# Neighbour lists of the first half moved into layer 1, and four tiles instead of six in the first phase

## The chip, the cores and the metric

The kernel runs on one core of one Trainium2 chip. The metric is the device time of one execution in microseconds (us); the time of a kernel is the median of its runs. A profile is one execution that the hardware profiler recorded; its span runs from its first to its last instruction, and the execution's own time is a little longer.

## The reference: two layers over one graph

There are N = 4096 nodes with 512 features each, and one dense matrix `adj` (4096 x 4096, float32), of which under 1% is not zero (each entry, its mirror and the diagonal).

```python
# layer 0
h = maximum(layernorm(x), 0)
d = where(rowsum > 0, rowsum ** -0.5, 0)          # rowsum = adj.sum(axis=1)
x = x + relu((d[:, None] * adj * d[None, :]) @ h @ W0 + b0)
# layer 1
h = maximum(layernorm(x), 0)
e = leaky_relu(h @ W @ a[:F] + (h @ W @ a[F:]).T, 0.2)
att = softmax(where(adj > 0, e, -1e12), axis=1)
neg = -softmax(where(adj > 0, -e, -1e12), axis=1)
x = x + elu(concatenate([att @ h, neg @ h], axis=1) @ wtrans)
```

Layer 0 is a dense product. Layer 1 needs, for each row, only the rows of `h` that `adj` marks.

## The kernel before

**Layer 0, first phase (lines 922 to 983).** The 4096 rows are 32 tiles of 128. For each row tile j the kernel loads the row of `adj` (four pieces of 512 KB, on SP's queue) and sums it for `d` (three pieces on ScalarE, one on VectorE), normalizes and transposes the tile of x (`turn_x`, matmuls at line 648), multiplies it by W0 (`project`, line 679) and scales it into `y0[j]`, which stays in SBUF. In the same loop a few columns of the result are accumulated plainly: `GROUPS[0]` names the first tile and the number of tiles, six before, and `multiply` (line 852) does one 128x512 matmul for each of them and each j. Each of these tiles holds one of the eight PSUM banks through the phase; the projections and transposes use those left. The part of `adj_t` for these columns is loaded for each j.

**Layer 0, the other groups (`group`, lines 1032 to 1083).** Each entry (i0, n) of `GROUPS` after the first is n tiles of output, over 16 steps `jp` of two row tiles. Here the product of 2x2 blocks is formed with seven products in place of eight (line 893, 128x256 matmuls): per step and pair of tiles seven matmuls. The left-hand sums of blocks of `adj_t` are made on VectorE (`sum_at`, lines 880 to 883). The results of the group before are finished during the first steps (`finish0`): residual, layer norm, the two scalar products s and t of a row for layer 1, and the row written to DRAM, on GpSimd's and ScalarE's queues, into eight tables, so that layer 1 can gather from each of them.

**Masks and lists.** Layer 1 works on 64 blocks of 64 rows, two blocks to a pair. `pack` turns each loaded part of `adj_t` into a byte mask, writes it to the tables behind the rows, and leaves a flag for each block and neighbour. A group in `EARLY` has its part of `adj_t` loaded and masked beforehand, in the group that the dictionary names by its index, and once more for its own product. `make_lists(g)` makes the neighbour lists of one half of the blocks (g = 0 or 1). `make_keys` transposes flags on TensorE (line 552) and forms sort keys and counts. Then 60 rounds (`list_round`: an eight-fold maximum at line 391 and a replacement at line 393) sort them, `make_places` finds where each list begins, and 24 joins (line 413, indirect DMAs from GpSimd) write pieces to DRAM. `deal` reads them back as indices with three DMAs. The units of this work stand in two queues in Python, `listing` and `joining`, from which `step(jp)` takes a few in each step of a group: that sets the order of the program around the change. Each engine takes its instructions in the order in which the program issues them to it.

**Layer 1 (`sparse_layer1`, lines 1236 to 1380).** The first pair, 16, is worked on within the last group of layer 0. For the others a loop over 62 blocks does, at block k, the `product` of block k (14 matmuls of 128x512, two records each in the profile, line 1296), asks for the gathers of a pair two further on (`gather`, line 451: 22 indirect DMAs on GpSimd in chunks of 8, 6 and 8), makes the weights of block k + 2 on VectorE and ScalarE (lines 463 to 493), turns the block before, and at every second block multiplies a finished pair by `wtrans` (`finish1`, line 1319). There are two sets of three buffers for gathered rows. The blocks begin with the second half's (pair 17 on), so that the lists of half g = 1 are needed first and those of g = 0 only from pair 0 on, after 15 pairs. `judge` compares counts, and on a bad verdict a dense version of layer 1 would run; it does not here.

Of the kernel before, what the change touches and what calls it, by code (L numbers as in the profile page):

```python
# [8 lines left out]
F32 = mybir.dt.float32  # L9
# [3 lines left out]
BF16 = mybir.dt.bfloat16  # L13
AF = mybir.ActivationFunctionType
ALU = mybir.AluOpType
# [4 lines left out]
P = 128  # L20
IB = 512


GROUPS = ((26, 6), (16, 4), (20, 4), (0, 4), (4, 4), (8, 4), (12, 4), (24, 2))

EARLY = {(24, 2): (2,), (12, 4): (3,), (8, 4): (4,)}
PAIR0 = 16
# [232 lines left out]
def gcn_gat_kernel(  # L260
# [159 lines left out]
    def deal(g):  # L420

        src = lst_dram[g].rearrange("(b n) o -> b (n o)", n=STR)
        k = 0
        for n in CHUNKS:
            nc.gpsimd.dma_start(
                out=idx[g][:, :, k : k + n],
                in_=src[:, k * P : (k + n) * P].rearrange("b (p k) -> p b k", k=n),
            )
            k += n

    def mean_var(pool, xt, name, pin):
# [14 lines left out]

    def gather(gt, n, a):

        c = sum(CHUNKS[:a])
        for k in range(CHUNKS[a]):  # L450
            nc.gpsimd.indirect_dma_start(  # L451
                out=gt[:, k, :],
                out_offset=None,
                in_=table[2 * n // RPT],
                in_offset=bass.IndirectOffsetOnAxis(
                    ap=idx[n // NH][:, n % NH, c + k : c + k + 1], axis=0
                ),
            )

    def scores(s, z, t):  # L460
# [53 lines left out]

    late_mask = ctx.enter_context(sbuf(name="late_mask", bufs=1, side="right"))
    late_m = late_mask.tile([P, EJ, TT * P], U8, name="late_m")
    with sbuf(name="y0", bufs=1) as y_pool, sbuf(name="wa", bufs=1) as wa_pool, sbuf(name="bits", bufs=4) as bits_pool, sbuf(name="small0", bufs=4) as small, ExitStack() as rest, ExitStack() as lists:
        list_pool = lists.enter_context(sbuf(name="list", bufs=1, side="right"))
        rank = list_pool.tile([P, EN], F32, name="rank")
        nc.gpsimd.iota(  # L520
            rank, [[-1, EN]], base=EN, channel_multiplier=0, allow_small_or_imprecise_dtypes=True
        )
        before = list_pool.tile([P, NE + 1, NH], F32, name="before")
        nc.gpsimd.memset(before[:, 0, :], 0.0)
        for e in range(NE):
            nc.vector.tensor_tensor(
                before[:, e + 1, :], before[:, e, :], ident[:, e * NH : (e + 1) * NH], ALU.add
            )
        start = list_pool.tile([NH, 1], F32, name="start")
        nc.gpsimd.iota(  # L530
            start, [[0, 1]], base=0, channel_multiplier=STR, allow_small_or_imprecise_dtypes=True
        )
        flags = [list_pool.tile([P, EJ * NE, 2 * NH], BF16, name=f"flags{g}") for g in range(2)]
        keys, lst = {}, {}
# [214 lines left out]
        def affine(y, acc, j):  # L749

            nc.vector.scalar_tensor_tensor(y, acc, d_all[:, j : j + 1], b_bc, ALU.mult, ALU.add)
            return y

        def new_y(work, j, k):
            if k < 0:
                return work.tile([P, F], F32, tag="y", name=f"y{j}", bufs=4)
            if k == 0:
                spare.append(make_pool.tile([P, 3, F], F32, tag="keys", name="spare"))
            return spare[0][:, k]

        def evict(i0, acc, work, _):

            return {
                i0 + k: affine(new_y(work, i0 + k, k - 3), a, i0 + k) for k, a in enumerate(acc)
            }

        def join_blocks(i0, n, acc, work, new_w):

            ys = {}
            for x in range(n // 2):  # L770
                p16, p23, p45, p7 = acc[x]
                j0, j1 = i0 + x, i0 + n // 2 + x
                ys[j0], ys[j1] = y, v = [new_y(work, j, -1) for j in (j0, j1)]
                w = new_w(f"w{j0}")[:, :H]
# [209 lines left out]
        pending = (GROUPS[0], partial(evict, i0, acc))  # L984
        listing, joining, spare = [], [], []

# [16 lines left out]

        def judge():

# [26 lines left out]
        def group(b, work, at_pool, sum_pool, step, prod, n_h=2):  # L1032
# [4 lines left out]
            (p0, pn), take = pending  # L1037
            order = [p0 + k for k in ((0, 2, 1, 3) if b > 1 else range(pn))]
            ats, sums = {}, {}
# [14 lines left out]
            for jp in range(NP):  # L1054
# [10 lines left out]
                multiply_blocks(acc, n, jp, ats[jp], sums[jp])  # L1065
                if (i0, n) not in EARLY:
                    pack(bits_pool, i0, 2 * jp, ats[jp])
# [23 lines left out]
        with sbuf(name="work0", bufs=2) as work, sbuf(name="sums", bufs=3) as sum_pool, sbuf(name="at", bufs=6) as at_pool:  # L1091

            def prod(name):
                return work.tile([P, F], F32, tag="q", name=name, bufs=1)

            for b in range(1, len(GROUPS) - 1):

                def step(jp):
                    if jp == 2 and b in (3, 5):
                        make_lists((1, 0)[b == 5])  # L1100
                    for _ in range((2, 3)[b == 6] if jp != 2 else 0):
                        if listing:
                            listing.pop(0)()
                    if joining:
                        joining.pop(0)()

                group(b, work, at_pool, sum_pool, step, prod)
            while listing:
                listing.pop(0)()
            while joining:  # L1110
                joining.pop(0)()
        lists.close()
        late = ctx.enter_context(sbuf(name="late", bufs=1, side="right"))
        late_h = late.tile([P, n_late, ROW_W], F32, name="late_h")
# [4 lines left out]
        with sbuf(name="work2", bufs=2) as work, sbuf(name="sums2", bufs=2) as sum_pool, sbuf(name="at2", bufs=4) as at_pool, sbuf(name="scratch", bufs=1) as scratch, sbuf(name="pair", bufs=1) as pair:  # L1119
# [96 lines left out]

            group(len(GROUPS) - 1, work, at_pool, sum_pool, step, row_tile, 4)
            k = late0 % EJ
# [12 lines left out]
            for r in blocks:  # L1231
                late_product0(r)
            verdict = judge()


    def sparse_layer1():
        with ExitStack() as pools:

            def pool(name, bufs):
                return pools.enter_context(sbuf(name=name, bufs=bufs))  # L1240
# [4 lines left out]
            tmp, small, p_pool = pool("tmp", 1), pool("small1", 2), pool("p", 3)  # L1245
            work, ut_pool, wt_pool = pool("work1", 2), pool("ut", 2), pool("wt", 1)
            warm = small.tile([P, 1], F32, tag="warm", name="warm", bufs=1)
            nc.scalar.activation(warm, sign, AF.Exp)
            wt_sb = wt_pool.tile([P, 2 * FC, F], F32, name="wt_sb")
            s_pool = pool("s", 2)  # L1250
            gath, wgt, us, uts, srow = {}, {}, {}, {PAIR0: ut0}, {}

            def load_s(k):
# [4 lines left out]
                )  # L1258

            def gather1(n, a):  # L1260
                k = pairs.index(n)
                gt = g_pools[k % 2, a].tile([P, CHUNKS[a], ROW], I32, tag="g", name=f"g{a}_{n}")
                gather(gt, n, a)
                gath.setdefault(n, []).append(gt)
# [94 lines left out]
            )  # L1359
            for k, r in enumerate(order):  # L1360
                product(r)
                if k % 6 == 1 and k // 6 < len(later):
# [12 lines left out]
                if k == 2:  # L1375
                    finish1(PAIR0)
                if k % 2 and k > 1:
                    finish1(order[k - 3] // 2)
# [44 lines left out]
```

## Time and profile before

| | us |
|---|---|
| median of 3 runs (lowest, highest) | 2101.34 (2098.91, 2105.48) |
| the profiled execution | 2098.72 |
| its span | 2096.8 |
| TensorE busy | 1996.2 (95%) |
| VectorE busy | 1120.1 (53%) |
| ScalarE busy | 511.3 (24%) |
| GpSimd busy | 917.0 (44%) |
| first phase of layer 0 ends at | 334 |
| last group of layer 0 starts at | 971.5 |

Engines are named PE (TensorE), PEld (its weight loads), DVE (VectorE), ACT (ScalarE), POOL (GpSimd) and SP (the queue for DMAs). In the view by stretches a line gives the stretch, its length, and the busy time of each engine with the number of instructions that began there; PEclk is the clock granted to TensorE as a share of full speed. In a timeline a line gives start, duration, engine, line of the kernel, operation, output <- inputs, sizes and how many alike follow each other; in brackets stands how long the engine was idle before, and what ended it. In the view of waits a line gives engine and line, what it waited for, and then the total in us, the number of times and the longest.

### The profile page before, as it was taken

How to read it: one execution, taken by the hardware profiler on the slowest of the kernel's cores; microseconds unless marked ns; L12 is line 12 of the kernel's file. 1: busy time of each engine (PE TensorE's matmuls, PEld its weight loads, DVE VectorE, ACT ScalarE, POOL GpSimd, SP SyncE). 2: the span in 40 equal slices, each digit the busy share in tenths (PEclk: the TensorE clock that was granted, in tenths of full speed). 3: DMA queues.
4: the chain of work that ended last, by engine and by line, in shares of the span. 5: the costliest groups of instructions: out<-in, count | busy, mean ns of one | idle time of the engine just before them, and what ended most of it. 6: DMA issues, size and time to landing. Idle time of an engine off the chain costs nothing.

```text
span 2096.8 us, 20037 instructions
## 1 busy us (share of the span) xinstructions
PE 1996.2 (95%) x6456; PEld 1180.1 (56%) x6456; DVE 1120.1 (53%) x2805; ACT 511.3 (24%) x876; POOL 917.0 (44%) x980
## 2 busy tenths in 40 slices
PE   7999999999899879899879999999999999999998
PEld 3444446888787768788634444444444444444443
DVE  5444436563798458945545455554544544445441
ACT  4645612222332310000111222212212211121120
POOL 2010001111113320220577777777777777776740
PEclk9999999999999999999989999999999999999999
DMA  9988927887887776383689888888888888888850
GB/s 381 366 307 321 371 71 252 290 284 220 307 281 256 253 222 238 90 270 111 204 265 302 255 288 293 263 287 254 271 240 274 261 258 245 242 247 236 240 161 22
DMA packets 188040, 524.11 MB, mean 250 GB/s; under 512 B 25235, under 2 KB 34419, under 8 KB 187926
## 3 DMA queue, kind: packets, MB, share of 16 engines
q0 software_dynamic: 71296, 275.22, 42.2%
q1 hardware_dynamic: 86640, 192.78, 27.1%
q10 hardware_dynamic: 29990, 54.75, 7.4%
q8 instruction: 52, 0.85, 0.2%
q14 instruction: 62, 0.51, 0.1%
HBM read 430.83 MB, written 102.92 MB: 255 GB/s over the span
## 4 chain that ended last, share of the span: by engine, by line
PE 49%; DVE 6%; DMA 5%; POOL 3%; issue 2%; ACTq 1%; ACT 0%; DVEq 0%; SPq 0%; POOLq 0%
PE u L1296 32%; PE o L1319 10%; PE p L893 5%; POOL g L451 3%; DMA g<-table,idx 2%; DVE keys L393 1%; PE tp L508 1%; DVE lst L391 1%; DMA table<-h 1%; DMA ld<-li,off 1%; DMA at<-in_adj_t 1%; PE u L1174 1%; ACTq L443 1%; DVE prod L816 0%; DMA table<-m 0%
## 5 line engine op out<-in xcount | busy, mean ns | idle before, releaser
L451 POOL DMA_INDIRECT g<-table,idx x704 | 747.8, 1062 | 259.9 <-issue 186.4
L1296 PE MATMUL u<-g,p 128*128 128x512 f32 x1736 | 762.4, 596 | 9.8 <-DVE p L482 9.8
L1296 PEld LDWEIGHTS u<-g,p 128*128 128x128 f32 x1736 | 326.0, 191 | 397.5 <-issue 362.9
L463 DVE TENSOR_TENSOR z<-g,s 128x512 f32<-128x512 f32 (+1 forms) x124 | 77.5, 625 | 390.4 <-DMA g<-table,idx 357.8
L893 PE MATMUL p<-t,sums 128*128 128x256 f32 x832 | 249.0, 384 | 13.3 <-DVE sums L881 13.3
L893 PE MATMUL p<-y,sums 128*128 128x256 f32 x832 | 252.0, 385 | 6.5 <-DVE sums L883 6.5
L893 PE MATMUL p<-y,at 128*128 128x256 f32 x832 | 252.4, 386 | 4.9 <-DMA at<-in_adj_t 4.6
L1319 PE MATMUL o<-wt_sb,ut 128*128 128x512 f32 x512 | 225.1, 592 | 0.5 <-ACT ut L512 0.5
L473 ACT ACTIVATE p<-z 128x896 f32<-128x896 f32 (+2 forms) x136 | 116.1, 905 | 268.3 <-DVE z L469 248.1
L893 PEld LDWEIGHTS p<-t,sums 128*128 128x128 f32 x832 | 159.6, 193 | 37.5 <-DVE sums L881 15.5
L893 PEld LDWEIGHTS p<-y,sums 128*128 128x128 f32 x832 | 160.7, 193 | 29.9 <-DVE sums L883 7.3
L852 PE MATMUL acc<-y,at 128*128 128x512 f32 x384 | 174.9, 593 | 2.4 <-ACT y L702 2.4
L482 DVE SCALAR_TENSOR_TENSOR p<-g,p 128x384 f32<-128x384 uint8 (+1 forms) x256 | 143.2, 620 | 63.3 <-ACT p L473 62.3
L893 PEld LDWEIGHTS p<-y,at 128*128 128x128 f32 x832 | 159.3, 193 | 30.7 <-ACT m L716 5.0
L727 POOL DMA_DIRECT2D table<-m x71 | 54.3, 766 | 248.5 <-ACT m L716 145.5
L1319 PEld LDWEIGHTS o<-wt_sb,ut 128*128 128x128 f32 x512 | 94.8, 190 | 107.8 <-issue 106.9
L716 ACT ACTIVATE m<-at 128x1024 uint8<-128x1024 f32 (+1 forms) x110 | 105.2, 987 | 183.8 <-DMA at<-in_adj_t 137.3
L893 PE MATMUL p<-t,at 128*128 128x256 f32 x416 | 126.3, 386 | 18.5 <-DVE w L776 17.7
L1305 ACT ACTIVATE us<-u,rl 128x512 f32<-128x512 f32 x62 | 42.5, 686 | 414.7 <-issue 217.4
L679 PE MATMUL yp<-w_sb,hx_t 128*128 128x512 f32 x256 | 123.2, 627 | 17.3 <-ACT y L702 14.8
L852 PEld LDWEIGHTS acc<-y,at 128*128 128x128 f32 x384 | 70.5, 190 | 80.5 <-issue 77.4
L413 POOL DMA_INDIRECT ld<-li,off x48 | 43.2, 901 | 159.8 <-DMA ld<-li,off 115.8
(182 smaller groups left out, 1718.5 us busy)
## 6 DMA issues: line engine op xcount, KB each, us to landing
at<-in_adj_t SPq DMA_DIRECT2D x136, 512.0 KB, 5.1
ar<-in_adj SPq DMA_DIRECT2D x128, 512.0 KB, 8.4
table<-h ACTq DMA_DIRECT2D x182, 258.0 KB, 5.8
table<-m POOLq DMA_DIRECT2D x55, 256.0 KB, 5.6
at<-in_adj_t SPq DMA_DIRECT2D x32, 384.0 KB, 5.0
g<-table,idx POOLq DMA_INDIRECT x704, 4.3
xr<-in_x SPq DMA_DIRECT2D x32, 256.0 KB, 3.5
x<-x1d SPq DMA_DIRECT2D x32, 256.0 KB, 5.2
```

What stands on the lines that cost most here:

```text
L413: return nc.gpsimd.indirect_dma_start(out=lst_dram[g][:, :], out_offset=bass.IndirectOffsetOnAxis(ap=off[g][:, e, c : c + 1], axis=0), in_ ...
L451: nc.gpsimd.indirect_dma_start(out=gt[:, k, :], out_offset=None, in_=table[2 * n // RPT], in_offset=bass.IndirectOffsetOnAxis(ap=idx[n // ...
L463: return nc.vector.tensor_tensor(z, t.to_broadcast([P, n, RB]), s.unsqueeze(1).to_broadcast([P, n, RB]), ALU.add)
L473: i = nc.scalar.activation(p[:, :, g, :], z, AF.Exp, scale=(1.0, -1.0)[g])
L482: nc.vector.scalar_tensor_tensor(e, m, 0.0, e, ALU.is_gt, ALU.mult)
L679: nc.tensor.matmul(yp, hx_t[j][:, c * P : (c + 1) * P], w0_sb[:, c, :], start=c == 0, stop=c == FC - 1,)
L716: nc.scalar.activation(m, at, AF.Sign)
L727: nc.gpsimd.dma_start(out=rows_of(t, e)[:, c:, ROW_W + (a - t * TT) * P // 4 : ROW_W + (b - t * TT) * P // 4], in_=masks[i0][:, c:, (a - i ...
L852: nc.tensor.matmul(a, at[:, 0, it * P : (it + 1) * P], y0[j], start=j == 0, stop=j == NJ - 1)
L893: i = nc.tensor.matmul(out, left[:, x * P : (x + 1) * P], right, start=jp == 0 and first, stop=jp == NP - 1 and (final or not first),)
L1296: nc.tensor.matmul(u, p[:, k0 + k].rearrange("p g c -> p (g c)"), gt[:, k, :F].bitcast(F32), start=k0 + k == 0, stop=k0 + k == nk - 1,)
L1319: nc.tensor.matmul(po, ut[:, g, c, :], wt_sb[:, g * FC + c, :], start=g == 0 and c == 0, stop=g == 1 and c == FC - 1,)
```

## The change

- `GROUPS` begins with four tiles, (28, 4), for six, and the tiles 26 and 27 become a block group of their own, (26, 2), between (16, 4) and (20, 4). The order of finishing the first four tiles and `new_y` follow from that.
- `EARLY` keeps only (24, 2), in the fourth entry of `GROUPS` counted from 0 as index 3. The early loads for (12, 4) and (8, 4) go.
- `make_lists(1)` is issued in group index 4, which is (0, 4), as before in a group of the same tiles, two units in each step.
- `make_lists(0)` is issued in layer 1 after the product of block k = 3; its constant tables are made once more in memory of layer 1. From k = 4 on five units of the list are issued per block.
- The joins of half 0 are issued singly between gathers: `gather` calls `join_next` ahead of the third and seventh gather of a chunk of eight and ahead of the third of a chunk of six. What is left is issued at k = 23. The gathers then keep their place in the program.
- `judge` moves from the end of layer 0 to k = 40. The pool for s is opened ahead of that for `wtrans`, the flags of half 0 have a pool that outlives layer 0, and the last group of layer 0 has three buffers for h in place of four.

```diff
-GROUPS = ((26, 6), (16, 4), (20, 4), (0, 4), (4, 4), (8, 4), (12, 4), (24, 2))
-
-EARLY = {(24, 2): (2,), (12, 4): (3,), (8, 4): (4,)}
+GROUPS = ((28, 4), (16, 4), (26, 2), (20, 4), (0, 4), (4, 4), (8, 4), (12, 4), (24, 2))
+
+EARLY = {(24, 2): (3,)}
...
-    def gather(gt, n, a):
+    def gather(gt, n, a, between=None):

         c = sum(CHUNKS[:a])
         for k in range(CHUNKS[a]):
-            nc.gpsimd.indirect_dma_start(
+            if between and k % 4 == 2:
+                between()
+            i = nc.gpsimd.indirect_dma_start(
                 out=gt[:, k, :],
...
+            if between:
+                tc.keep_in_program_order(i)
...
-            order = [p0 + k for k in ((0, 2, 1, 3) if b > 1 else range(pn))]
+            order = [p0 + k for k in ((0, 2, 1, 3) if b > 1 and pn == 4 else range(pn))]
...
-                if (i0, n) not in EARLY:
+                if (i0, n) not in EARLY and 2 * jp % nj == 0:
                     pack(bits_pool, i0, 2 * jp, ats[jp])
...
-                    if jp == 2 and b in (3, 5):
-                        make_lists((1, 0)[b == 5])
-                    for _ in range((2, 3)[b == 6] if jp != 2 else 0):
+                    if jp == 2 and b == 4:
+                        make_lists(1)
+                    for _ in range(2 if jp != 2 else 0):
                         if listing:
                             listing.pop(0)()
...
-            group(len(GROUPS) - 1, work, at_pool, sum_pool, step, row_tile, 4)
+            group(len(GROUPS) - 1, work, at_pool, sum_pool, step, row_tile, 3)
...
-            verdict = judge()
...
-            work, ut_pool, wt_pool = pool("work1", 2), pool("ut", 2), pool("wt", 1)
+            work, ut_pool, s_pool, wt_pool = pool("work1", 2), pool("ut", 2), pool("s", 2), pool("wt", 1)
...
+            def join_next():
+
+                if joining:
+                    tc.keep_in_program_order(joining.pop(0)())
+
             def gather1(n, a):
                 k = pairs.index(n)
                 gt = g_pools[k % 2, a].tile([P, CHUNKS[a], ROW], I32, tag="g", name=f"g{a}_{n}")
-                gather(gt, n, a)
+                gather(gt, n, a, join_next if 3 < current < 30 else None)
...
             for k, r in enumerate(order):
+                current = k
                 product(r)
...
+                if k == 3:
+                    lates.close()
+                    make_pool = pool("make1", 1)
+                    rank, before, start = list_tables(make_pool)
+                    make_lists(0)
+                if k > 3:
+                    for todo in listing[:5]:
+                        todo()
+                    del listing[:5]
+                if k == 23:
+                    while joining:
+                        joining.pop(0)()
+                if k == 40:
+                    verdict = judge(small)
```

## The prediction

> **What bounds the kernel now.** I read the stretches of the span first: the busy time of each engine in each stage, the granted clock, the share of the DMA engines and GB/s.
>
> ```profile
> core 0: us, PE busy (x) PEld busy (x) DVE busy (x) ACT busy (x) POOL busy (x), PEclk, DMA share, GB/s
> 25.00:100.00 75.00, 70.89 (x186) 32.00 (x187) 39.79 (x130) 46.47 (x99) 9.20 (x15) 1.00 1.00 378
> 100.00:250.00 150.00, 137.09 (x347) 62.31 (x346) 66.11 (x198) 82.57 (x174) 14.37 (x23) 0.95 0.91 332
> 250.00:334.00 84.00, 84.00 (x217) 37.27 (x216) 32.70 (x85) 22.64 (x40) 3.90 (x7) 1.00 0.40 133
> ...
> 430.00:528.00 98.00, 98.00 (x456) 85.82 (x455) 50.98 (x143) 26.77 (x38) 15.92 (x27) 1.00 0.79 256
> 528.00:643.00 115.00, 104.45 (x493) 90.01 (x491) 103.71 (x317) 38.19 (x43) 21.77 (x34) 0.97 0.85 285
> 643.00:765.00 122.00, 103.64 (x450) 87.88 (x450) 61.00 (x170) 30.57 (x36) 37.86 (x49) 0.92 0.80 256
> ...
> 1106.00:1500.00 394.00, 393.32 (x1023) 181.76 (x1024) 200.61 (x372) 82.45 (x139) 302.74 (x284) 1.00 0.87 276
> ```
>
> TensorE sets the pace nearly everywhere. The exceptions are the first 250 us (DMA share 0.91 to 1.00) and the groups that carry list work: 115 and 122 us, where an undisturbed group takes 98. In 528 to 643 DVE is busy 104 of 115 us.
>
> Next the timeline of PE, for the price of one matmul in each form and for the stalls:
>
> ```profile
> 239.34 2.74 PE L852 MATMUL acc<-y,at 128*128 128x512 f32 x6
> ...
> 242.35 2.74 PE L852 MATMUL acc<-y,at 128*128 128x512 f32 x6
> 244.97 3.70 PE L679 MATMUL yp<-w_sb,hx_t 128*128 128x512 f32 x8
> ```
> ```profile
> 563.33 0.59 PE L893 MATMUL p<-y,sums 128*128 128x256 f32 x2
> 563.76 0.59 PE L893 MATMUL p<-y,at 128*128 128x256 f32 x2
> 570.40 1.22 PE L893 MATMUL p<-y,sums 128*128 128x256 f32 x2 [6.05 <-DVE sums L883]
> ```
> ```profile
> 1078.52 14.40 PE L1296 MATMUL u<-g,p 128*128 128x512 f32 x28 [9.47 <-DVE p L482]
> ...
> 1106.12 12.28 PE L1296 MATMUL u<-g,p 128*128 128x512 f32 x28 [0.35 <-DVE p L482]
> ```
>
> A matmul is two records. By start to start, six records of 128x512 take 2.57 us (0.859 us a matmul) and two of 128x256 take 0.432 us. A pair of tiles in a block group is therefore 16 steps x 7 x 0.432 = 48.35 us; a tile in the first phase is 32 x 0.859 = 27.5 us, so two are 55.0. In the second fence a lump of list work on DVE makes the sums late and PE stands 6.05 us; the next matmuls run at half pace. In the third, layer 1: from 1106 on PE is gapless, 32.24 us per pair of blocks.
>
> Last the waits, for what POOL does in its lists and gathers:
>
> ```profile
> DVE z L463 <- DMA g<-table,idx: 372.9, 82, 8.2
> ...
> POOL ld L413 <- DMA ld<-li,off: 115.8, 41, 5.9
> ```
>
> Each join in before waits for the one ahead of it.
>
> **What the Trainium skill says.** "TensorE: Matmul & The Clock Gate", Part 1 (What's actually happening): after an idle window of about 3.4 us the clock halves until about 3.4 us of steady work. The trace agrees: the granted clock was 0.5 for 3.4 to 10.2 us after each long stall. "DMA: Bandwidth & Descriptors", Anatomy of one DMA: a transfer from GpSimd has about 2.0 us fixed, mostly the receipt of its write. The joins took 2.0 to 6.8 us to land, median 4.3. The same page (Where 436 GB/s comes from) puts one core's HBM reading near 358 GB/s; here 378 was moved at share 1.00, and I use 378.
>
> **The change part by part.** The sum is made against the profiled execution: 2098.7 us, of which 2096.8 is span and 1.9 lies around it. It is 2.6 us under the median of 2101.3.
>
> *Before, in the same terms.* First phase to 334.3; six groups (twelve pairs of tiles) to 971.5, which is 580.2 pure plus 57 lost; then 1125.3 to the end.
>
> *First phase, four tiles for six.* A row tile costs PE 6 x 0.859 + 3.43 (projection, eight records) + 0.43 (transposes) = 9.02 us before, 7.30 after. From the first accumulation at 25.8: 25.8 + 32 x 7.30 - 8.2 (two projections and three transposes of the ramp lie earlier) + 3.6 (the weight rows at the end) = 254.8. The same sum for before is 309.8 against a real 334.3: 24.5 lost to late x tiles, to projections that wait for a PSUM bank, and to the clock after that. Four accumulators leave four banks, not two, which helps. But there is less PE work to hide loads behind: about 86 MB must come (adj 67.1, x 8.4, four columns of adj_t 8.4, masks out 2.1), 228 us at 378 GB/s and 259 at the 332 of 100 to 250. I keep 20 of the loss: end at 275. Bounds: 258 with PE nearly free of stalls, 300 if the loads pace it from 20 on at 307 GB/s.
>
> *Two tiles move to a block group (26,2):* +48.35 us; the groups ahead of (24,2) are now thirteen pairs, 628.4. With the first phase that is -55.0 + 48.35 in pure work, so -6.7: the small certain gain.
>
> *Lists of the first half leave layer 0; two re-loads of 8.4 MB of adj_t with their masks and writes leave too.* The 57 lost splits by group ends: about 0 in (16,4), 1.3 in (20,4), 18.7 in (0,4), 24.9 in (4,4), 14.0 in (8,4), 0 in (12,4). The 18.7 are the lump of keys (6.4), rounds that bound DVE (4.6), and the clock after each. The 24.9 are joins that hold POOL, so that table puts of the new rows come late, then ACT, then the sums (9.0), and adj_t loads late by 5.0 and 5.8. The 14.0 are the rounds of the first half. After: one set of rounds in (0,4) with fewer masks beside it, 12; its joins in (4,4) with less traffic, 8; none in (8,4); the new two-tile group opens with four tiles to finish in half the matmul time per step, 4; small remains 6.5. Together 30.5, taken between 20 and 50.
>
> *Layer 1 takes the lists on.* DVE is busy 25 of 50 us there. A round is at most 0.65 + 0.64 us, five per block of 16.1 us about 5: hidden under products, since masks end 8 us before their product at the fourth product, 15 at the ninth, about 32 late on. If that cover were gone, 60 rounds would be some 60 us. Two things are not hidden. (a) In PE's new order the eight key transposes stand behind the fourth product and wait for flags that DVE makes after the masks of a later block, about 1151 in before's time, where PE would be at 1143.5: 7.4 idle, 1 for the transposes, 3.4 for the clock. (b) The new order of the first pair's gathers completes chunk 0 at the twenty-first of 22 instead of the sixteenth; these go out 1.25 to 1.37 us apart, so its first product is some 6 us later, and 5 of it reach the gapless part. Together 17.5, between 5 and 35. The judge's matmul leaves the transition (nothing: PE waits for gathers there). The s buffers in other memory and three h buffers for four: nothing, as no row of the page waits on them; if they did, one load of 5.2 us.
>
> *Joins among gathers, on POOL.* 24 x (0.87 + 0.3) + 3 deals of 1.2 + 0.7 for the tables = 32.4 us. A pair's gathers take 22 x 1.37 = 30.1 of 32.24 us. The lead is 17.6 at the thirteenth product plus the 17.5 by which PE is now later, capped at about 32 by the two sets of buffers; 2.1 x 6 pairs = 12.8 are regained during the joins. 32 + 12.8 - 32.4 leaves 12: no stall, if a join finds the one ahead landed. The spacing is four gathers, some 6.6 us with the join, against 2.0 to 6.8 to landing: near, but enough for most.
>
> *Sum:* 275 + 628.4 + 30.5 + 1125.3 + 17.5 = 2076.7 span, + 1.9 = 2078.6, against 2098.7. On the median's scale + 2.6: 2081.
>
> **Rivals.** A measurement of this kernel tells about 0.3%, 6.3 us, from no change.
> - *Stall-free first phase* (end 258 instead of 275, from the freed banks): 2064, and 2053 if the groups lose only 20 as well. For it: PE has no gap after 250. Against: share 0.91 to 1.00 before that.
> - *Joins wait among the gathers.* If each join holds POOL for the landing of its forerunner, or of gathers ahead of it in the same queue, everything behind it on POOL is gathers, for which DVE's z and then PE wait. At 2 us each (a gather and a join land after about 4.3): 48 - 12 = 36 us stall, 2117, slower. It stalls from 0.5 us a join, and is slower than before from 1.6 us a join. Against: the spacing exceeds the median landing.
> - *The first phase stays with its loads* (end about 300) or the groups lose 50 again: 2101 to 2106, about no change.
>
> **How the numbers follow.** Forecast 0.52 (2062 to 2095, its own range); stall-free first phase 0.20; waiting joins 0.13; loads pace or losses stay 0.15. The range 2050 to 2112 takes in the second case and the fourth, and leaves out most of the third. Faster: 0.50 + 0.20 + 0.07 of the last two = 0.77; same 0.10; slower 0.13.
>
> **What would show it.** First phase: last plain matmul at 258 to 285, row tiles 7.3 us apart late in it. Groups: (0,4) at 105 to 115 us, (8,4) at 97. Layer 1: one PE gap of 5 to 9 us at the key transposes behind the fourth product, then 32.24 us per pair without a gap through the joins. The waits should show joins waiting for joins a few times in layer 1, at most 1 us, against 41 times and 115.8 us in all. Wrong if the first phase ends after 295, or PE waits for gathers between the thirteenth and twenty-sixth product.

## The result and the profile after

The changed kernel takes 2086.68 us (median of 5, 2085.44 to 2092.64); the kernel before takes 2101.34 beside it. The ratio is 0.9932, with a 95% interval of 0.9912 to 0.9952: faster by 0.7%. The forecast was 2081 with a range of 2050 to 2112. The profiled execution has a span of 2083.8 us, 13.0 less than the 2096.8 of before.

Two views of the changed kernel first. The stretches, with cuts at its own stage ends; the columns are those explained for before:

```profile
core 0: us, PE busy (x) PEld busy (x) DVE busy (x) ACT busy (x) POOL busy (x), PEclk, DMA share, GB/s
25.00:100.00 75.00, 68.34 (x183) 31.04 (x184) 41.93 (x144) 48.31 (x104) 7.94 (x13) 1.00 0.97 361
100.00:250.00 150.00, 141.11 (x380) 64.17 (x379) 71.84 (x218) 93.80 (x194) 11.35 (x19) 1.00 0.93 347
...
373.00:429.00 56.00, 50.92 (x228) 43.81 (x227) 30.66 (x96) 12.52 (x19) 10.05 (x19) 0.94 0.86 285
...
526.00:626.00 100.00, 98.19 (x476) 85.42 (x475) 93.79 (x295) 20.68 (x25) 16.38 (x26) 1.00 0.65 210
626.00:731.00 105.00, 99.67 (x451) 85.93 (x450) 62.23 (x177) 20.47 (x25) 30.67 (x41) 0.97 0.65 207
...
926.00:987.00 61.00, 53.28 (x226) 45.13 (x225) 35.52 (x99) 8.88 (x14) 26.65 (x32) 0.92 0.75 240
...
1065.00:1500.00 435.00, 416.54 (x1087) 192.09 (x1086) 258.71 (x597) 83.41 (x141) 332.06 (x313) 0.98 0.80 249
```

The first phase is over at 274.5 instead of 334.3. The group with list work, (0, 4), takes 100 us instead of 107 (525.9 to 626.4, before 530.6 to 637.9; the 115 of the prediction, 528 to 643, took in the first stall of the next group). But layer 1 is no longer gapless: in 1065 to 1500 PE is busy for 416.5 of 435 us, where before had 393.3 of 394. The waits of PE in 1090 to 1600 say at what, first in the changed kernel, then in before:

```profile
PE tp L513 <- ACT us L1329: 10.4, 4, 3.5
PE kp L573 <- DVE flag L571: 7.9, 1, 7.9
```
```profile
PE tp L508 <- ACT us L1305: 0.6, 1, 0.6
```

Before waits once at the transposes (`tp`), for 0.6 us, and not for flags. To compare the stages, I counted the block matmuls in both traces (224 to a pair of tiles), which puts the start of before's last group at 975.1, not at the 971.5 that I had read from the stretches; the six groups had lost 60.6, not 57. By the same count (0, 4) had lost 10.6, (4, 4) 23.6, (8, 4) 11.1 and (12, 4) 12.5; the prediction had 18.7, 24.9, 14.0 and 0, read at ends that lie some us off. Products are counted from 1, k from 0.

| us | before | after | after - before |
|---|---|---|---|
| first phase, to the first block matmul | 334.3 | 274.5 | -59.8 |
| groups ahead of (24, 2): matmuls | 580.2 (12 pairs) | 628.6 (13) | +48.4 |
| their losses | 60.6 | 22.8 | -37.8 |
| (24, 2) itself | 55.1 | 61.2 | +6.1 |
| its end to product 3 of layer 1 | 75.9 | 77.8 | +1.9 |
| product 3 to product 5 | 39.3 | 50.6 | +11.3 |
| product 5 to 17 | 194.1 | 194.5 | +0.4 |
| product 17 to 27 | 161.1 | 177.0 | +15.9 |
| the rest to the end | 596.2 | 596.9 | +0.7 |
| all (with rounding) | 2096.8 | 2083.8 | -13.0 |

So the list work taken out of layer 0 saved 37.8 us there, net of the new group's own loss, and cost 36.3 in the stages that follow.

### The profile page after: what moved, and what is told of

Read it like the earlier page. It is cut to its first block, busy times and chain, and to the rows that moved or that the text cites. A ratio compares the mean times of both kernels' runs of the same rounds, so it can differ in the third digit from the quotient of the medians.

```text
span 2083.8 us, 20393 instructions
## 1 busy us (share of the span) xinstructions
PE 1986.7 (95%) x6554; PEld 1195.9 (57%) x6554; DVE 1130.2 (54%) x2859; ACT 522.0 (25%) x885; POOL 926.8 (44%) x983
## 3 DMA queue, kind: packets, MB, share of 16 engines
q1 hardware_dynamic: 82160, 176.00, 24.9%
## 4 chain that ended last, share of the span: by engine, by line
PE 32%; POOL 8%; DMA 4%; DVE 4%; issue 4%; ACT 1%; DVEq 0%; POOLq 0%; ACTq 0%
PE u L1320 23%; PE o L1343 8%; POOL g L454 8%; DMA g<-table,idx 4%; PE tp L513 1%; DVE p L487 1%; DVE z L474 1%; DVE z L468 0%; POOL ld L413 0%; DVE keys L393 0%; ACT p L478 0%; DMA ld<-li,off 0%; DVE tree L492 0%; DVE lst L391 0%; PE cs L503 0%
## 5 line engine op out<-in xcount | busy, mean ns | idle before, releaser
L1320 PE MATMUL u<-g,p 128*128 128x512 f32 x1736 | 762.7, 597 | 16.6 <-DVE p L487 16.6
L468 DVE TENSOR_TENSOR z<-g,s 128x384 f32<-128x384 f32 (+1 forms) x124 | 77.4, 624 | 385.3 <-DMA g<-table,idx 352.8
L910 PE MATMUL p<-t,sums 128*128 128x256 f32 x896 | 267.1, 383 | 9.9 <-DVE sums L898 9.9
L910 PE MATMUL p<-y,at 128*128 128x256 f32 x896 | 269.2, 382 | 0.5 <-DMA at<-in_adj_t 0.4
L910 PE MATMUL p<-y,sums 128*128 128x256 f32 x896 | 269.3, 382 | 0.0
L910 PEld LDWEIGHTS p<-t,sums 128*128 128x128 f32 x896 | 171.6, 192 | 35.0 <-DVE sums L898 11.5
L910 PEld LDWEIGHTS p<-y,at 128*128 128x128 f32 x896 | 170.3, 191 | 26.9 <-issue 1.6
L910 PEld LDWEIGHTS p<-y,sums 128*128 128x128 f32 x896 | 171.8, 192 | 24.2 <-issue 0.4
L897 DVE TENSOR_TENSOR sums<-at 128x256 f32<-128x256 f32 x112 | 47.0, 419 | 198.6 <-PE p L910 191.0
L869 PE MATMUL acc<-y,at 128*128 128x512 f32 x256 | 120.9, 597 | 8.2 <-ACT y L723 8.2
L700 PE MATMUL yp<-w_sb,hx_t 128*128 128x512 f32 x256 | 117.1, 601 | 10.6 <-DVE hx_t L675 9.5
L690 ACT ACTIVATE ar<-ar 128x1024 f32<-128x1024 f32 x96 | 100.2, 1044 | 13.5 <-DMA ar<-in_adj 13.1
```

The costliest lines, as they stand in the source:

```text
L468: return nc.vector.tensor_tensor(z, t.to_broadcast([P, n, RB]), s.unsqueeze(1).to_broadcast([P, n, RB]), ALU.add)
L690: i = nc.scalar.activation(ar, ar, AF.Identity, accum_out=part[:, c : c + 1])
L700: nc.tensor.matmul(yp, hx_t[j][:, c * P : (c + 1) * P], w0_sb[:, c, :], start=c == 0, stop=c == FC - 1,)
L869: nc.tensor.matmul(a, at[:, 0, it * P : (it + 1) * P], y0[j], start=j == 0, stop=j == NJ - 1)
L910: i = nc.tensor.matmul(out, left[:, x * P : (x + 1) * P], right, start=jp == 0 and first, stop=jp == NP - 1 and (final or not first),)
L1320: nc.tensor.matmul(u, p[:, k0 + k].rearrange("p g c -> p (g c)"), gt[:, k, :F].bitcast(F32), start=k0 + k == 0, stop=k0 + k == nk - 1,)
```

## The experiments

Each edit is against the changed kernel unless it says otherwise. Only the groups, the reciprocal ahead, no joins and flags ahead ran on a chip that the record numbers 3, where before takes 2101.9. The others ran on chips numbered 4, 9 and 12, where before takes 2133.4, 2134.2 and 2131.6, and where in every kernel profiled PE stands in layer 1 for 19 us or more in 1090 to 1600 at waits for which the profile names no cause. The changed kernel was not run on these three chips, nor before profiled there, so of these runs I use ratios to before on the same chip, and compare gaps only among kernels that ran there.

**Only the groups (the kernel before, four tiles and (26, 2), lists where they were).**

```diff
-GROUPS = ((26, 6), (16, 4), (20, 4), (0, 4), (4, 4), (8, 4), (12, 4), (24, 2))
-EARLY = {(24, 2): (2,), (12, 4): (3,), (8, 4): (4,)}
+GROUPS = ((28, 4), (16, 4), (26, 2), (20, 4), (0, 4), (4, 4), (8, 4), (12, 4), (24, 2))
+EARLY = {(24, 2): (3,), (12, 4): (4,), (8, 4): (5,)}
...
-                    if jp == 2 and b in (3, 5):
-                        make_lists((1, 0)[b == 5])
-                    for _ in range((2, 3)[b == 6] if jp != 2 else 0):
+                    if jp == 2 and b in (4, 6):
+                        make_lists((1, 0)[b == 6])
+                    for _ in range((2, 3)[b == 7] if jp != 2 else 0):
```

> The kernel before with four tiles in the first phase and a group (26, 2) of its own, lists and early loads kept in layer 0 one group index later. Theory (the first phase is bound by PE and gives back about 60 us, of which the new group takes 48.4 and 6 to 8 of losses, while the list losses of some 58 us stay): first phase ends at 272 to 277, the time is 2093 to 2099. Rival (the gain of the change is all in the first phase): 2086 or less.

Measured: 2087.51 us, ratio 0.9938 (0.9920 to 0.9955). The first phase ends at 273.8, the groups lose 59.3, and from the last group to the end are 1122.4 us. The first phase came out as the theory had it. The time lies between the two expectations, since the losses did not rise by those of the new group: 59.3 in all, where I had expected 58 and 6 to 8 more. For the change it is clear all the same: this half of it gives a span of 2084.1, and the whole change gives 2083.8. All of the gain is here.

**Only the lists (six tiles in the first phase, no group (26, 2), and `new_y` with its spare tile as before).**

```diff
-GROUPS = ((28, 4), (16, 4), (26, 2), (20, 4), (0, 4), (4, 4), (8, 4), (12, 4), (24, 2))
-EARLY = {(24, 2): (3,)}
+GROUPS = ((26, 6), (16, 4), (20, 4), (0, 4), (4, 4), (8, 4), (12, 4), (24, 2))
+EARLY = {(24, 2): (2,)}
...
-                    if jp == 2 and b == 4:
+                    if jp == 2 and b == 3:
```

> The kernel before with only the lists of the first half moved to layer 1 (with s of layer 1 in other memory, the early loads for two groups gone, the judge later); six tiles in the first phase, no group (26, 2). Theory (the list move takes 35 to 40 us of losses out of the block groups and puts about as much into layer 1 and the last group): the twelve pairs of block groups end some 36 us earlier against the first phase, from there to the end some 33 to 38 us more; the time is 2096 to 2105, within 0.3% of before. Rival (both parts of the change gain): 2090 or less.

Measured: ratio 0.9983 (0.9965 to 1.0002), on chip 4: no difference that can be told. The twelve pairs lose 14.4 us from 335.5 to 930.1, some 46 less than before. By the ratio, what they save is spent later; how much of that is the lists can't be read here, since 33 us in 1090 to 1600 are waits without a named cause. This agrees with the other half.

**The reciprocal ahead.** The next question was the 15.9 us of products 17 to 27. The gap of 3.33 us in the changed kernel, on PE and then on DVE:

```profile
1309.81 0.28 PE L503 MATMUL cs<-ones,total 128*128 128x1 f32 x2
...
1322.63 12.26 PE L1320 MATMUL u<-g,p 128*128 128x512 f32 x28
1338.22 0.66 PE L513 MATMUL tp<-ident,us 128*128 128x128 f32 x4 [3.33 <-ACT us L1329]
```
```profile
1328.55 0.57 DVE L468 TENSOR_TENSOR z<-g,s 128x384 f32<-128x384 f32 x1 [7.12 <-DMA g<-table,idx]
1329.15 1.09 DVE L474 SCALAR_TENSOR_TENSOR z<-z 128x896 f32<-128x896 f32 x1
1331.26 2.23 DVE L487 SCALAR_TENSOR_TENSOR p<-g,p 128x512 f32<-128x512 uint8 x4 [1.02 <-ACT p L478]
...
1336.07 0.16 DVE L505 RECIPROCAL rl<-cs 128x1 f32<-128x1 f32 x1
...
1337.20 0.16 DVE L506 TENSOR_TENSOR rl<-rl,sign 128x1 f32<-128x1 f32 x1
```

The column sum for product 17 (k = 16) was there at 1310. Its reciprocal `rl` stands on DVE behind the weights of the block two further on (k = 18), whose z waits 7.12 us for a gather that the joins have put off. ACT needs `rl` to scale the product (1337.48), PE needs that for the transposes. The weights themselves are in time. The edit puts `rl` first:

```diff
...
                 for gt, k, n in parts(r):
-                    scores(s, z[:, k : k + n], gt[:, :, ROW_T : ROW_T + 1].bitcast(F32))
+                    i = scores(s, z[:, k : k + n], gt[:, :, ROW_T : ROW_T + 1].bitcast(F32))
+                    if pin:
+                        tc.keep_in_program_order(i)
...
-                    weights(order[k + 2])
+                    weights(order[k + 2], k > 3)
```

> Only the order on DVE in layer 1 differs from the changed kernel: the z of block k+2 is put behind the reciprocal rl of block k. Theory (rl, ready since the start of product k, stands on DVE behind a z that waits for gathers made late by the joins; so the scaled u and its transposes are late): the three gaps of PE at the transposes (3.3, 3.5, 3.3 us) and the half clock after them vanish, the stretch from the 17th to the 27th product takes 161 to 164 us instead of 177.0, and the time is 2070 to 2076. Rival (the lead of the gathers is used up and the weights themselves are late): the order of rl changes nothing, the stretch stays at 175 or more and the time at 2085 or more.

Measured: 2077.62 us, ratio 0.9880 (0.9863 to 0.9897), by the intervals faster than the changed kernel, and than only the groups on the same chip (0.9938, 0.9920 to 0.9955): with this order the list move does gain, some 10 us. Products 17 to 27 take 170.1: 6.9 of the 15.9 us are gone. The theory is right but not complete, as three gaps (2.9, 2.5, 1.3) stay. ACT shows why:

```profile
1368.33 1.79 ACT L478 ACTIVATE p<-z 128x896 f32<-128x896 f32 x2 [15.35 <-DVE z L474]
1370.03 0.67 ACT L1331 ACTIVATE us<-u,rl 128x512 f32<-128x512 f32 x1
```

The product ended at 1355.0 and `rl` was ready at 1353.8; the scaled copy stands behind exponentials that wait for the same late z. It is the same stall, one engine on.

**The reciprocal and the copy ahead**, twice. As above, and `exps(z, p, pin=pin)` in place of `exps(z, p)`.

> As the run with rl ahead of the z of block k+2, and on ACT the scaled copy of product k ahead of the exponentials of block k+2. Theory (the gaps left in that run, 2.9, 2.5 and 1.3 us, come from the copy standing on ACT behind exponentials that wait for the same late gathers): the gaps at the transposes vanish, 17th to 27th product takes 161 to 163 us instead of 177.0 (170.1 with rl alone), the time is 2069 to 2073. Rival (the weights are truly late): the stretch stays at 168 or more, and the time at 2077 or more.

> The same kernel as the run with rl and the copy ahead, once more: in that run PE stood for short times inside its products with nothing to wait for, in a stretch without joins too, and this hid the size of the gain. Theory: as there, no gap at the transposes after the key transposes; 17th to 27th product in 161 to 163 us, the time 10 to 16 us under the changed kernel, 2069 to 2076 if the kernel before takes 2101. Rival (the weights are late): 168 or more, 2077 or more.

Measured, on chips 4 and 9: ratios 0.9965 (0.9949 to 0.9981) and 0.9987 (0.9971 to 1.0003). Waits of PE in 1090 to 1600, first run:

```profile
PE u L1322 <- issue: 20.7, 18, 2.5
PE o_ps L596 <- issue: 8.7, 6, 1.9
```

No wait of the transposes for ACT is left, but that shows nothing here: only the lists (chip 4) and two tiles (chip 9) have none either, with the order of the changed kernel. The first lines of only the lists in the same stretch:

```profile
PE o L1349 <- issue: 21.1, 19, 2.2
PE u L1326 <- issue: 5.2, 5, 1.5
```

Where PE stands so often by itself, the gathers are further ahead of it: at product 17 by 33.8 us in only the lists, against 20.7 in the changed kernel (from the end on POOL of the last gather that the block needs). Products 17 to 27 took 181.9 and 180.9 (185.6 in only the lists, 176.9 in two tiles), so the sizes that were to tell the theories apart can't be read. Whether the second pin gains or costs is open.

**No joins.** The kernel leaves out the 24 joins of layer 1, and the deal reads the other half's lists, so for half of the output the gathers fetch the rows of other neighbours, as many as before.

```diff
-        src = lst_dram[g].rearrange("(b n) o -> b (n o)", n=STR)
+        src = lst_dram[1].rearrange("(b n) o -> b (n o)", n=STR)
...
+                while joining and joining[0].func is join:
+                    joining.pop(0)
                 if joining:
...
```

> The 24 joins of layer 1 are left out, and the deal takes the lists of the other half, so half of the output is computed from wrong neighbours. Theory (joins on POOL delay the gathers): the three gaps at the transposes vanish, 17th to 27th product in 161 us instead of 177.0, the time about 2070. Rival (list rounds on DVE hold up rl): the gaps stay, since the rounds stay, and the time is about 2085.

Measured: 2070.97 us in one run. The stretch 1310 to 1487 in this kernel and then in the changed one:

```profile
1310.00:1487.00 177.00, 177.00 (x465) 82.00 (x463) 90.50 (x170) 37.87 (x63) 137.13 (x129) 1.00 0.86 275
```
```profile
1310.00:1487.00 177.00, 166.70 (x422) 76.45 (x421) 81.45 (x150) 34.67 (x59) 136.12 (x131) 0.97 0.81 246
```

Without joins PE is gapless there and products 17 to 27 take 161.1, as before. The list rounds on DVE, which stayed, cost next to nothing (one gap of 1.2 us, earlier). In this one run the joins are worth 15.7 us, about the loss of that stretch.

**Tables on DVE.** What takes POOL's lead? Not waits between joins: in 1100 to 1420 of the changed kernel a join waited once for another, 1.3 us. The waits of POOL there hold a line that I had not priced:

```profile
POOL rank L531 <- issue: 8.4, 1, 8.4
POOL ld L413 <- issue: 6.1, 20, 0.3
...
POOL ld L413 <- DMA ld<-li,off: 1.3, 1, 1.3
```
```profile
1101.94 0.95 POOL L454 DMA_INDIRECT g<-table,idx  x1 [0.30 <-issue]
1111.25 0.56 POOL L531 IOTA rank<- 128x512 f32 x1 [8.36 <-issue]
```

The iota that makes the rank table a second time runs for 0.56 us, but POOL stands for 8.36 before it. The trace has a MODIFY_POOL_CONFIG of the same line at 1103.0, and nothing after it until the iota. The Trainium skill, "GPSIMD Engine Reference", 2.1 Instruction dispatch, has this: the first call of a newly loaded routine pays a load of about 6 us (5.95 measured) that no instruction in a profile shows. The trace agrees with the place but not the size: POOL stood 7.2 to 8.9 us before the iota, in eight traces. A second iota at 1130.25, behind more gathers but with no MODIFY_POOL_CONFIG ahead of it, came without any standing. The edit makes the table by doubling on DVE:

```diff
...
+            nc.vector.memset(rank[:, 0:1], float(EN))
+            n = 1
+            while n < EN:
+                nc.vector.tensor_scalar(
+                    rank[:, n : 2 * n], rank[:, :n], -float(n), None, ALU.add
+                )
+                n *= 2
...
-                    rank, before, start = list_tables(make_pool)
+                    rank, before = tables_on_dve(make_pool)
```

> The rank and prefix tables of layer 1 made on DVE, so that POOL has no iota among the gathers (before it POOL stood 8.4 us). Theory (these 8.4 us are a part of the lead that the joins then lack): the gathers of the pairs with joins go out some 8 us earlier against their products, the three gaps shrink to under 4 us in all, 17th to 27th product in 161 to 168 us instead of 177.0, and the key transposes keep their gap of about 8; the time is 2072 to 2080. Rival (the lead is capped by the buffers, so nothing of the 8.4 us is left when the joins begin): 175 or more, 2085 or more.

Measured, chip 4: ratio 0.9900 (0.9863 to 0.9937), which can't be told from the 0.9932 of the changed kernel. PE has no wait for ACT at the transposes, but only the lists, with the iota, has none on that chip either. The key transposes wait 2.4 us, where I had expected about 8 (1.1 in only the lists). In products 17 to 27, 176.9, there are again waits without a named cause. That POOL stands for the iota is measured; what these 8 us cost TensorE is not shown.

**All joins late.** The gathers keep their order, but no join is asked for between them; what the scheduler does with the flush at k = 23 is to set the joins in ones, twos and threes wherever a list is ready.

```diff
-                gather(gt, n, a, join_next if 3 < current < 30 else None)
+                gather(gt, n, a, (lambda: None) if 3 < current < 30 else None)
```

> All 24 joins of layer 1 in a burst at k = 23, none between gathers. Theory (a join waits for the landing of the one ahead, 4 to 5 us with its own issue, and only gathers in between hide this): the burst holds POOL for 90 to 130 us, PE waits for gathers for 50 to 100 us, the time is 2135 to 2185. Rival (joins hardly wait): the burst takes 28 us, POOL's lead covers it, and without joins ahead of it the three gaps go; the time is about 2072.

Measured, one run on chip 4: 2150.71 us, against 2133.38 for before there. It was not one burst, so the numbers of neither side apply as they stand. But joins in direct sequence do wait. Waits of POOL in 1190 to 1400:

```profile
POOL ld L413 <- DMA ld<-li,off: 29.3, 11, 4.7
```

That is 2.7 us at each of 11 waits, against 1.3 us once when four to twelve gathers lie between. PE waits 13.8 us for ACT at the transposes and 9.3 for DVE at the column sums, as in no other run on that chip. Over 24 joins that is 1.2 us each, and this run is 17 us slower than the median of before. So joins can wait for each other; what that costs in time isn't settled by one run. With single joins between gathers they hardly wait.

**Flags ahead.** The two flag operations are issued ahead of the weights of block k = 5; the products of the expectation are counted from 0.

```diff
...
+                if k == 3:
+                    lates.close()
+                    make_pool = pool("make1", 1)
+                    early_bits = make_bits(0)
                 if k + 2 < len(order):
-                    weights(order[k + 2])
+                    weights(order[k + 2], k == 3)
...
```

> Only the two flag operations of the first half are made ahead of the weights of block 5 on DVE. Theory (PE stands at the key transposes only because the flags queue behind weights that wait for gathers): the gap of 7.9 us and the half clock after it fall to under 1.5 us together, product 4 follows product 2 by 40 to 42 us instead of 50.6, the time is 2075 to 2080. Rival (the stall moves on, to the keys that wait for the rank table from POOL, or to the gathers): product 4 to 17 takes the 9 us back, the time is 2084 or more.

Measured: 2088.57 us, ratio 0.9935 (0.9916 to 0.9953): no gain, as the rival said. The key transposes wait for 0.3 us and product 5 starts 40.2 us after product 3; then DVE stands:

```profile
1131.04 0.18 DVE L541 TENSOR_TENSOR before<-before,ident 128x16 f32<-128x16 f32 x1 [11.90 <-POOL before L539]
...
1131.46 0.29 DVE L498 TENSOR_TENSOR total<-tree 128x128 f32<-128x128 f32 x1
```

The prefix table wants a memset of 0.1 us from POOL, which stands behind the gathers of a pair. The total of a block's weights is behind it on DVE, and PE waits 11.9 us for its column sum. The stall moved to the next thing that shared POOL with the gathers.

**Two tiles in the first phase.** `(30, 2)` and `(26, 4)` for `(28, 4)` and `(26, 2)`.

> The changed kernel with two tiles in the first phase, (30, 2), and a group (26, 4) in place of (26, 2). PE's work of the first phase is then 199.8 by the same sum (254.8 with four tiles), its loads some 81 MB, 213 us at 378 GB/s. Theory (with four tiles PE sets the end, with two the loads do): the first phase ends at 230 to 248, so 26 to 44 us are saved and 48.4 spent, the new group loses 0 to 2 in place of 7.6; the time is 2082 to 2104, no faster than the changed kernel by more than 4 us. Rival (PE sets the end still): the phase ends at 220 or less, and the time is 2076 or less.

Measured, chip 9: ratio 1.0155 (1.0133 to 1.0176). The first phase ends at 273.0, where it ended with four tiles; both sides were wrong. Stretches of this kernel, and the same hundred of the changed kernel:

```profile
100.00:200.00 100.00, 79.51 (x204) 36.06 (x203) 44.68 (x148) 55.07 (x114) 8.72 (x15) 0.91 0.82 283
200.00:250.00 50.00, 43.22 (x112) 18.01 (x110) 19.55 (x56) 31.88 (x63) 1.66 (x4) 1.00 0.93 325
```
```profile
100.00:200.00 100.00, 94.83 (x258) 43.42 (x256) 48.73 (x155) 60.62 (x129) 9.28 (x16) 1.00 0.96 356
```

With four tiles PE (95%) and the DMA engines (0.96) are both near their end. With two, neither is in this hundred, and the row tiles come no faster: loads, statistics and scaling of each wait for each other (VectorE 54.5 us for x tiles, weight loads 29.4 us for the scaled y between 60 and 240). Which link sets that pace isn't settled. With two tiles in place of four there was nothing to gain.

**All mends**, in two versions: `rl` and the copy ahead, flags ahead, tables on DVE, the row of s in the two-tile group at step 12 for 8. The second holds the flags' place for the first half alone, and has in the last group:

```diff
                     gather0(0)
-                    weights0(blocks[0])
+                if jp == 13:
+                    weights0(blocks[0], True)
```

> All mends together: rl and the copy ahead, the flags of the first half ahead of the weights of block 5, the tables on DVE, and in the two-tile group the row of s turned at step 12 instead of 8. Theory (each takes away its own stall): no gap at the key transposes (11 us with the clock), none at the later transposes (16), 5 to 8 less in (26, 2); the time is 2052 to 2062 if the kernel before takes 2101, ratio 0.977 to 0.982. Rival (the stalls hide behind each other, since the gathers bound that part of layer 1): 2066 or more.

> The kernel with all mends, with two corrections: the early flags hold their place on DVE for the first half alone (in the run with all mends they held it in (0, 4) too, and PE stood 7.9 us there), and in the last group the z of pair 16 stands behind the last sums of the group on DVE. Theory (the stalls are separate, each with its own cause): (0, 4) loses 4 to 9 us instead of 12.7, the last group 7 to 10 instead of 12.8 in the changed kernel, no gaps at the key transposes and at the later transposes; the ratio to the kernel before is 0.971 to 0.980. Rival (the gathers bound the start of layer 1, so what is saved ahead of them is waited for again): 0.983 or more.

Measured, chips 9 and 12: ratios 0.9923 (0.9907 to 0.9939) and 0.9928 (0.9912 to 0.9945), by the numbers on the rivals' side (0.983 or more). One mend works where it is: (26, 2) loses 0.5 us instead of 7.6. No transposes wait for ACT and the key transposes wait 2.8 and 3.3 us, but kernels without these mends wait no longer on those chips. The last group lost 19.7 and 16.8 us; the six other runs on those chips lost about 17 to 20 there, so its mend isn't seen to gain. With the waits without a named cause, the rivals' reason, gathers as the bound, isn't shown either. Whether all mends together beat the changed kernel, or the first of them alone, is open.

## Why the prediction was right, and where it was not

**First phase: right, 275 against 274.5.** The 7.30 us a row tile and the kept loss of 20 us gave the number. Its reason is weaker than it looked: the run with two tiles ends at 273.0 although its PE sum is 199.8. The loss is not a remainder of stalls that happened to stay: by that run this loop ends at about 273 even when PE has 55 us less to do. So the 20 that I kept were the right number in part by luck, and the rival of a stall-free phase at 258 was, by the same run, out of reach.

**Groups: 658.9 forecast, 651.4 measured.** The matmuls are exact (628.6). Losses are 22.8 instead of 30.5: (0, 4) 3.8 for 12, with a gap of 1.8 us where the lump of keys had made one of 6.0; fewer masks, the reason in the prediction, isn't it, since only the groups kept these masks and lost 2.3 there, and what else it was is open; (4, 4) 8.4 for 8; (26, 2) 7.6 for 4, from the row of s that is turned at step 8 while the fourth tile's rows wait for table writes (PE stands 5.1 us, then the clock; turned at step 12 the group lost 0.5); the others 3.0 for 6.5.

**Key transposes: right, 11.3 against 11.8**, of which 7.9 is the wait for the flags (7.4 forecast). What I did not see is the mend's trap, the prefix table that waits on POOL.

**First product: 5 forecast, 1.9 measured.** PE's wait for the weights of the first product did grow, from 9.5 us to 16.6. But PE was at that wait 5.2 us sooner after its group's end, mostly because an earlier wait for DVE was 0.8 us instead of 4.2. The sum had no term for that.

**Joins: this is the step that failed, "leaves 12: no stall".** The lead was mis-sized. Take as lead the time from the end on POOL of the last gather that a block needs to the start of its product. At product 5 it was 34.7 us, against 18.3 before: 16 longer, much as the prediction had it. By product 13, when one join had gone out ahead of that gather, it should have been some 14 longer (32 for 17.6). It was 24.4 against 26.1; before first, then the changed kernel:

```profile
1247.94 0.95 POOL L451 DMA_INDIRECT g<-table,idx  x1 [0.30 <-issue]
...
1275.03 12.26 PE L1296 MATMUL u<-g,p 128*128 128x512 f32 x28
```
```profile
1220.12 0.95 POOL L454 DMA_INDIRECT g<-table,idx  x1 [0.30 <-issue]
...
1245.50 12.26 PE L1320 MATMUL u<-g,p 128*128 128x512 f32 x28
```

Two things had eaten it. The iota and the standing before it took 8.9 us, where 0.7 was priced for all tables. And the gathers of the pairs of products 9 and 11 took 35.0 and 34.3 us, where before's took 30.6 and 29.9; they ran while DVE made the list rounds (1125 to 1243). That the rounds slow them isn't tested. The joins then cost POOL 29.9 us with their issue, near the 28.1 forecast; with the deals and the tables it was 43.3 for 32.4.

A lead is not usable to zero either: the weights of block k + 2 have to be done not when product k + 2 starts, but some 4 us before product k + 1 ends, as `rl` and the scaled copy of product k stand behind them in order. From the trace that is about 12 us earlier (4, and some 8 for transposes and the product with `wtrans`), an estimate. In before, a lead of 20.7 at product 7 was just enough (the transposes waited 0.6 us). For products 16 to 24 the changed kernel has 19.2 to 21.7, stalls included, and the run without joins 25.4 to 34.2. The three gaps are 10.1 us, and with the half clock after them 15.9.

The prediction's sign of being wrong, PE waiting for gathers between the thirteenth and twenty-sixth product, came true by way of DVE and ACT. The rival of waiting joins named the right resource and the wrong trigger: joins waited for each other once, 1.3 us. (In before they landed in 1.9 to 7.1 us, median 3.3; the median of 4.3 in the prediction is that of the gathers.)

**The last group: +6.1, not forecast.** A gap of 3.9 us at 974.8, where the sums on DVE stand behind the z of pair 16 that waits 8.1 us for its gathers, and the clock after it. Before, the same wait was 5.7 us and cost PE 0.35.

The sum came out 7.1 us low in span: 18.7 us too little for the end, against 7.5 too much for the groups, 3.6 of the misread start of the last group that stayed in the base, and 0.5 in the first phase. That 2081 came near is therefore in part luck: errors of both signs cancel. The first phase and the new group, -59.3 and +48.4 in the forecast and -59.8 and +48.4 measured, are nearly the whole of the gain; the list move, which I had put at -26.5 for the groups' losses and +17.5 for layer 1, came out at nothing.

## What to carry to other kernels

Work that is moved under a busy engine has to be costed on every in-order queue that it shares: here an operation of 0.16 us, a reciprocal, was the one that stalled TensorE, because it stood behind a wait for the delayed gathers. A lead between producer and consumer is used up where the first small operation behind the producer is due, not where the consumer starts. And two halves of a change are best run apart: one of them was all of the gain, and the other began to gain only when the reciprocal was put first.

## What the runs showed of the hardware that was not expected

- An iota on GpSimd behind a MODIFY_POOL_CONFIG among indirect DMAs cost 7.2 to 8.9 us of standing beside its own 0.56 us; one without it cost none, as above.
- The 22 gathers of a pair took 34 to 35 us in the changed kernel while DVE made list rounds, and 30 to 31 in before at the same products. The cause wasn't tested.
- Indirect writes to one DRAM tensor with four to twelve gathers in between waited once, 1.3 us; the same in ones, twos and threes 11 times, 29.3 us.
- On chips 4, 9 and 12 TensorE stood in stretches with gathers at waits for which the profile names nothing (20.7 us inside the products of one stretch of 510 us), and before took 2132 to 2134 us instead of 2102. What it waits for then wasn't found.
